# Moving softmax weights by small copies within SBUF, and splitting the keys' rotary product between GpSimd and an accumulating DMA

## The chip, the cores and the metric

The kernel runs on one core of a Trainium2 chip. The core has TensorE (PE, matrix products into PSUM), VectorE (DVE), ScalarE (ACT), GpSimd (POOL) and SyncE (SP), which here only issues DMAs. Each engine takes its instructions in the order in which they stand in its own queue; semaphores order the engines among each other. The metric is the time of one execution on the device in microseconds, and the median over the runs is what is compared. All arithmetic is float32, apart from the attention masks.

## What is computed

The input is x, 2 sequences of 2048 tokens of 128 features. Four residual layers follow each other, each on a layer norm of x:

```python
x = x + attention_a(layernorm(x))   # softmax over the queries' axis of x xT, 2048 x 2048 per sequence
x = x + ffn(layernorm(x))           # two transformer layers
x = x + attention_b(layernorm(x))   # one weight per token, from similarity of q and k
x = x + ffn(layernorm(x))           # the same two transformer layers again
```

The change lies in `ffn`. Each of its two layers has eight heads of 64 features with windows of 64 tokens, and then a gated feed-forward of width 341. Cut to what matters:

```python
q, k, v = split(shift_token(x) @ wqkv)
q, k = l2norm(q) * qs, l2norm(k) * ks
q = q * cos * scale + rotate_half(q) * sin * scale
k = k * cos / scale + rotate_half(k) * sin / scale
sim = (8 * q) @ kT over own and previous window, masked
x = x + (softmax(sim) @ v) @ wo
x = x + (a * gelu(g)) @ w2 + b2     # a, g = split(layernorm(shift_token(x)) @ w1 + b1)
```

`rotate_half` swaps the halves of a head's features (the sign is in the table). The l2 norm is a factor per token and head, so it may be applied after the rotation.

## The kernel before

A call `op(engine, cost, fn, r=..., w=..., late=...)` (class `Program`, line 102) records one operation with what it reads and writes; nothing is issued yet. At the end `Program.run` (line 127) lays all operations out: it keeps a clock per engine, advances it by the costs written in the calls and by `TAIL`, a delay until a result counts as there, and gives each engine the ready operation with the lowest number, shifted by `late`. Buffers are handed out in the same pass from pools of fixed size (`sizes`, line 322): an operation is only placed when its buffers are free. The outcome is one fixed order per engine; the chip follows it whatever the real durations are. A DMA on SyncE's queue that waits for data therefore holds back the DMAs behind it.

Attention a of both sequences comes first (`first_norm`, `first_attention`). Then four passes of the transformer run, two repetitions for each of the two sequences, as a chain of ticks (class `Block`): a pass has 16 blocks of 128 tokens per layer, and the second layer follows the first at a distance of 6 blocks. In all there are 4 x 2 x 16 = 128 calls of `Attention.block`, and 32 feed-forwards on 512 tokens.

One call of `block` does this, with the lines of the profile:

- Line 551: SyncE loads the block's table of cosines and sines (256 KB) from DRAM. There are three buffers for tables.
- Line 559: TensorE projects q and k for 128 tokens into two banks of PSUM, `pq[0]` and `pq[1]`; line 566 projects v, and line 567 (ScalarE) copies v to SBUF. Lines 569 and 573: SyncE moves v's halves so that each window and its predecessor lie in one buffer.
- Line 582: ScalarE squares each bank. Lines 583 and 584: VectorE multiplies each bank by the cosines (into `t1`) and by the sines (into `t2`), so four products of 128 x 512 per block.
- Lines 587 to 593: sums of squares, and the reciprocal norm; lines 394 to 397 are its Newton step on GpSimd.
- Line 591: GpSimd adds `t2`, halves swapped, to `t1` (128 x 1024). Line 597: GpSimd multiplies by the norm.
- Lines 606 and 607: VectorE transposes q into `qT` and k into `kring`, a ring of three blocks of keys. Line 628: TensorE multiplies queries with their 96 keys. Where the window begins before the ring's first column, the 96 keys lie in two pieces and each product is issued as two. Line 637 adds the masks.
- Lines 649 to 666: the softmax; line 666 (GpSimd) scales the weights. Line 677: VectorE transposes them in squares of 32 into `xp`.
- Line 686: four DMAs write `xp` into a DRAM buffer `far`, each 32 partitions to three row blocks. Line 691: one DMA reads `far` back into `pT` (512 KB). There the weights stand with the keys in the partitions; what the four DMAs never write in `far` was set to zero at the start (`clear`, line 517).
- Line 702: TensorE multiplies with v; line 709 (ScalarE) copies out; line 715 is the output projection of two blocks, and lines 721 and 722 (VectorE) add it.

Of the kernel before, what the change touches and what calls it, by code (L numbers as in the profile page):

```python
# [72 lines left out]
class Program:  # L73
# [6 lines left out]
    TAIL = {"PE": 0.28, "DVE": 0.2, "ACT": 0.25, "POOL": 0.19, "SP": 2.0}  # L80
# [195 lines left out]
def hybrid_kernel(ctx: ExitStack, tc: tile.TileContext, I, out):  # L276
# [37 lines left out]
    kring = [fixed([P, 4, R * P], f"kring{l}") for l in range(DEPTH)]  # L314

    def vec(i, rows=P):
# [7 lines left out]
        "w": (1024, 0), "c": (512, 12), "v": (VW, 6), "v0": (VW, 5), "tab": (TW, 3),  # L324
        "s0": (514, 2), "s1": (514, 3), "s2": (514, 2), "s3": (514, 2), 
        "n": (64, 7), "m": (16, 12), "row": (P, 4),
# [3 lines left out]
    scratch = ctx.enter_context(tc.tile_pool(name="scratch", bufs=1, space=bass.MemoryType.DRAM))  # L330
    slots["far"] = [scratch.tile([4 * P, 256], F32, name=f"far{i}") for i in range(8)]
# [4 lines left out]
    for b in range(B):  # L336
# [5 lines left out]
        "xn0": [("w", part[4]), ("w", part[5])],  # L342
        "xn1": [("w", part[6]), ("w", part[7])],
        "xnT0": [("w", part[8]), ("w", part[9])],
# [9 lines left out]
    def load(dst, key, src):  # L354
        op("SP", load_time(dst), lambda: sp.dma_start(out=dst, in_=src), w=[key], late=121)
# [5 lines left out]
    def load_x():  # L361
        c = len(x_tok)
        xt = buf("c")
        x_tok.append(xt)
        op(
            "SP", 2.0,
            lambda: sp.dma_start(out=xt().rearrange("p (n d) -> p n d", d=C), in_=x_rows[:, c * BPC : (c + 1) * BPC, :]),
            w=[xt],
        )
# [20 lines left out]
    def newton(v, r, rows, n, src):  # L390

        a = buf(src)
        A, V, Q = (lambda: a()[0:rows, 0:n]), (lambda: v()[0:rows, 0:n]), (lambda: r()[0:rows, 0:n])
        op("POOL", 0.22, lambda: po_.tensor_tensor(A(), Q(), Q(), ALU.mult), r=[r], w=[a], late=30)
        op("POOL", 0.22, lambda: po_.tensor_tensor(A(), A(), V(), ALU.mult), r=[v, a], w=[a], late=-30)
        op("POOL", 0.22, lambda: po_.tensor_scalar(A(), A(), -0.5, 1.5, ALU.mult, ALU.add), r=[a], w=[a], late=61)
        op("POOL", 0.22, lambda: po_.tensor_tensor(Q(), Q(), A(), ALU.mult), r=[r, a], w=[r])
# [13 lines left out]
    def first_norm(b, xn, xnT):  # L411
        for c in range(NCH):
# [9 lines left out]
            op("DVE", dve(512), lambda xg=xg, mean=mean: dv.tensor_reduce(row(mean), xg(), AX.X, ALU.add), r=[xt], w=[mean], late=56)  # L422
            op("DVE", 0.17, lambda mean=mean: dv.tensor_scalar(row(mean), row(mean), 1.0 / C, None, ALU.mult), w=[mean])
            op("DVE", dve(512), lambda xg=xg, ng=ng, mean=mean: dv.tensor_tensor(ng(), xg(), wide(mean), ALU.subtract), r=[xt, mean], w=[(xn, c)])
            op("ACT", act(512), lambda sq=sq, nf=nf: ac.activation(sq()[:, 0:CH], nf(), AF.Square), r=[(xn, c)], w=[sq])
            op("DVE", dve(512), lambda s3=s3, v=v: dv.tensor_reduce(row(v), s3(), AX.X, ALU.add), r=[sq], w=[v], late=84)
            op("DVE", 0.17, lambda v=v: dv.tensor_scalar(row(v), row(v), 1.0 / C, LN_EPS, ALU.mult, ALU.add), w=[v])
            op("ACT", 0.25, lambda v=v, r=r: ac.activation(row(r), row(v), AF.Ln), r=[v], w=[r], act="E", late=69)
            op("ACT", 0.25, lambda r=r: ac.activation(row(r), row(r), AF.Exp, scale=-0.5), w=[r], act="E", late=-36)
            newton(v, r, P, BPC, "m")  # L430
            op("DVE", dve(512), lambda ng=ng, r=r: dv.tensor_tensor(ng(), ng(), wide(r), ALU.mult), r=[r], w=[(xn, c)], late=-175)
            pt = transposes(BPC, (xn, c), lambda k, c=c: xn()[:, c * CH + k * P : c * CH + (k + 1) * P])
            op("ACT", act(512), lambda pt=pt, c=c: ac.copy(xnT()[:, c * CH : (c + 1) * CH], pt()), r=[pt], w=[(xnT, c)], late=-108)
            pt = transposes(BPC, xt, lambda k, xt=xt: xt()[:, k * P : (k + 1) * P])
            gc = b * NCH + c
            op("ACT", act(512), lambda pt=pt, gc=gc: ac.copy(xT[:, gc * CH : (gc + 1) * CH], pt()), r=[pt], w=[(xT_, gc)], late=-78)

    def first_attention(b, xn, xnT):
# [6 lines left out]
        for m in range(NBLK):  # L445
            group, z, xs = m // BPC, buf("m"), buf("row")
            e = [buf("e" if j <= group else "c" if j < NCH - 1 else "er") for j in range(NCH)]
            for j in range(group):
# [6 lines left out]
                op("PE", 0.115 * BPC, turned, r=[ident_] + [right[j * BPC + k, group] for k in range(BPC)], w=[pt], claim=[e[j]], late=-150)  # L455
                op("DVE", dve(512), lambda pt=pt, z=z, j=j: dv.tensor_reduce(z()[:, j : j + 1], pt(), AX.X, ALU.add), r=[pt], w=[(z, j)])
                op("ACT", act(512), lambda pt=pt, x=e[j]: ac.copy(x(), pt()), r=[pt], w=[e[j]])
            for j in range(group, NCH):
                sc = buf("p1")
                op("PE", pe(512), lambda sc=sc, m=m, j=j: pe_.matmul(out=sc(), lhsT=xnT()[:, m * P : (m + 1) * P], rhs=xnT()[:, j * CH : (j + 1) * CH], start=True, stop=True), r=[(xnT, group), (xnT, j)], w=[sc], claim=[e[j]], late=-79)  # L460
                op("ACT", act(512) + 0.25, lambda sc=sc, x=e[j], z=z, j=j: ac.activation(x(), sc(), AF.Exp, bias=shift, accum_out=z()[:, j : j + 1]), r=[sc], w=[e[j], (z, j)], act="E", late=-203)
                if j > group:
                    right[m, j] = e[j]
            op("DVE", 0.16, lambda z=z: dv.tensor_reduce(z()[:, 4:5], z()[:, 0:NCH], AX.X, ALU.add), w=[z])
            op("DVE", 0.17, lambda z=z: dv.reciprocal(z()[:, 4:5], z()[:, 4:5]), w=[z], late=-98)
            op("DVE", 0.3, lambda z=z, xs=xs, m=m: dv.tensor_scalar(xs(), xn()[:, m * P : (m + 1) * P], z()[:, 4:5], None, ALU.mult), r=[z, (xn, m // BPC)], w=[xs], late=-239)
            for j in range(NCH):
                op("PE", pe(512), lambda x=e[j], xs=xs, m=m, j=j: pe_.matmul(out=acc[j](), lhsT=xs(), rhs=x(), start=(m == 0), stop=(m == NBLK - 1)), r=[e[j], xs], w=[acc[j]], late=-32)  # L468
        for j in range(NCH):
            gc = b * NCH + j  # L470
            cols = xT[:, gc * CH : (gc + 1) * CH]
            op("DVE", dve(512), lambda cols=cols, j=j: dv.tensor_tensor(cols, acc[j](), cols, ALU.add), r=[acc[j]], w=[(xT_, gc)], late=-4)


    def center(src, keys):
# [3 lines left out]
        op("PE", pe(512), lambda: pe_.matmul(out=mp(), lhsT=meanw, rhs=src(), start=True, stop=True), r=keys, w=[mp], claim=[d, sq], late=-33)  # L479
        op("DVE", dve(512), lambda: dv.tensor_tensor(d(), src(), mp(), ALU.subtract), r=keys + [mp], w=[d], late=36)  # L480
        op("ACT", act(512), lambda: ac.activation(sq()[:, 0:CH], d(), AF.Square), r=[d], w=[sq], late=-31)
        op("PE", pe(512), lambda: pe_.matmul(out=vp(), lhsT=meanw, rhs=sq()[:, 0:CH], start=True, stop=True), r=[sq], w=[vp], claim=[r])  # L482
        op("ACT", act(512) + 0.1, lambda: ac.activation(r(), vp(), AF.Ln, bias=eps), r=[vp], w=[r], act="E", late=27)
        op("ACT", act(512), lambda: ac.activation(r(), r(), AF.Exp, scale=-0.5), w=[r], act="E", late=-27)
# [4 lines left out]
    def halo(s, before):  # L489
        if before is None:  # L490
            op("POOL", 0.15, lambda: po_.memset(s()[64:128, 0:1], 0.0), w=[(s, "h")], late=-49)
        else:
            op("POOL", 0.15, lambda: po_.tensor_copy(s()[64:128, 0:1], before()[64:128, CH : CH + 1]), r=[(before, BPC - 1)], w=[(s, "h")])
# [8 lines left out]
    def state_norm(gc, s, before):  # L502
        d, r = center(lambda: xT[:, gc * CH : (gc + 1) * CH], [(xT_, gc)])
        op("POOL", pool(512), lambda: po_.tensor_tensor(s()[0:64, 0:CH], d()[0:64, :], r()[0:64, :], ALU.mult), r=[d, r], w=[(s, k) for k in range(BPC)], late=-49)
        op("POOL", pool(512), lambda: po_.tensor_tensor(s()[64:128, 1 : CH + 1], d()[64:128, :], r()[64:128, :], ALU.mult), r=[d, r], w=[(s, k) for k in range(BPC)], late=-146)
# [7 lines left out]

    nought = Fixed()

    def clear():
        for far in slots["far"]:
            for a in range(4):
                z0 = a * P + (0 if a % 2 else 96)
                op("SP", 0.4, lambda far=far, z0=z0: sp.dma_start(out=far[z0 : z0 + 32, :], in_=I["zero"]), w=[(nought, z0)], late=7)  # L520

# [3 lines left out]
    def tables():  # L525
        for i in range(NBLK):
            raw = buf("tab")
            op("SP", 0.4, lambda i=i, raw=raw: sp.dma_start(out=raw(), in_=I["rot"][i]), w=[raw])
            for l in range(DEPTH):
# [6 lines left out]
                    r=[raw, qs_], w=[tab], late=35,  # L536
                )
                op("SP", 0.4, lambda l=l, i=i, tab=tab: sp.dma_start(out=turns[l][i], in_=tab()), r=[tab], w=[turns_[l][i]])

    class Attention:  # L540
# [4 lines left out]
        def block(self, i, s, s_out, before_out):  # L545
# [5 lines left out]
            op("SP", 0.4, lambda: sp.dma_start(out=tab(), in_=turns[l][i]), r=[turns_[l][i]], w=[tab], late=-48)  # L551
# [9 lines left out]
            for k in range(2):  # L561
                op("PE", 0.97, lambda k=k: project(k), r=keys_of(s, q) + [wqkv_], w=[pq[k]], claim=[sq, t1, t2], late=-24)
# [3 lines left out]
            op("PE", 0.885, lambda: pe_.matmul(out=pv(), lhsT=h(), rhs=wqkv[:, l, 2 * INNER : 3 * INNER], start=True, stop=True), r=keys_of(s, q) + [wqkv_], w=[pv], claim=[v])  # L566
            op("ACT", act(512), lambda: ac.copy(v(), pv()), r=[pv], w=[v], late=-123)  # L567
            old = self.v
            op("SP", 0.4, lambda: sp.dma_start(out=v0()[64:128, :], in_=v()[0:64, :]), r=[v], w=[(v0, 0)], late=71)
# [540 lines left out]
```

## Time and profile before

| | |
|---|---|
| median of 3 runs | 1640.41 us (1636.79 to 1644.73) |
| the profiled execution | 1623.37 us, of which the span is 1621.3 us |
| mean granted TensorE clock | 0.96 |
| busy: PE / DVE / ACT / POOL | 1482.7 / 1341.4 / 960.0 / 1072.2 us |
| share of the span | 91% / 83% / 59% / 66% |
| instructions: PE / DVE / ACT / POOL | 21659 / 2464 / 2426 / 1308 |
| DMA, all queues | 208.55 MB in 183542 packets, mean 129 GB/s |

The span runs from the first to the last instruction. Busy times are of one execution. The end of a matmul is modelled in the profile and consecutive matmuls overlap, so a busy TensorE is not one at its peak. A row of a group gives line, engine, operation, output and input, their shapes and the count, then the busy time and the mean duration of one, then the idle time before it with what ended it. "SPq" is SyncE's queue: its rows are the times in which DMAs are issued, not moved; the DMA list gives size and the median time from issue to landing. The first attention takes the first 200 us or so, the passes of the transformer nearly all the rest.

### The profile page before, as it was taken

Reading aid. Unit: us, or ns where it says so; the run is one execution under the profiler, and the core shown is the slowest. Engines: PE = TensorE matmul, PEld = TensorE weight load, DVE = VectorE, ACT = ScalarE, POOL = GpSimd, SP = SyncE. Lnnn points to the kernel's source line nnn. Section 1 sums busy time; section 2 is a strip of 40 time slices with the busy share of each in tenths; the row PEclk is TensorE's granted clock in tenths of the full one; section 3 lists DMA queues with packets and bytes.
Section 4 is the critical chain, followed back from the end, with each engine's and each line's share of the span. In section 5 each row is a group of like instructions: output and inputs, shape, how many; then the busy total and the mean of one; then the engine's idle time right before and its main releaser. Section 6 shows DMA issues by size and latency. Waiting matters only on the chain.

```text
span 1621.3 us, 53049 instructions
## 1 busy us (share of the span) xinstructions
PE 1482.7 (91%) x21659; PEld 844.0 (52%) x21659; DVE 1341.4 (83%) x2464; ACT 960.0 (59%) x2426; POOL 1072.2 (66%) x1308
## 2 busy tenths in 40 slices
PE   7999997989999999699999899799999999899875
PEld 4454554545555555355555464455555555555543
DVE  4533378799999899989998999989999989899772
ACT  6453455566666566465666666556666756566652
POOL 3440147578697767758687757758697877786561
PEclk9999998999999999799999999789999999999997
DMA  5540025455464543235555443255555555555432
GB/s 191 163 148 1 14 67 142 111 150 156 136 172 124 156 134 97 84 98 167 144 144 164 118 137 105 58 153 152 147 153 169 154 147 157 139 152 153 133 97 60
DMA packets 183542, 208.55 MB, mean 129 GB/s; under 512 B 18474, under 2 KB 143876, under 8 KB 183300
## 3 DMA queue, kind: packets, MB, share of 16 engines
q1 hardware_dynamic: 183300, 205.18, 44.4%
q8 instruction: 170, 2.79, 0.7%
q14 instruction: 72, 0.59, 0.1%
HBM read 111.78 MB, written 61.87 MB: 107 GB/s over the span
## 4 chain that ended last, share of the span: by engine, by line
PE 60%; DVE 17%; DMA 9%; POOL 5%; issue 4%; SPq 2%; ACT 2%; POOLq 0%; DVEq 0%; ACTq 0%
PE pp L751 9%; PE pp L559 9%; PE pp L702 6%; PE pp L628 6%; PE pp L715 5%; PE pp L468 5%; PE pp L566 5%; PE pp L776 4%; DMA arena<-far 3%; PE pp L482 2%; PE pp L479 2%; PE pp L460 2%; DMA right<-far 2%; DVE b_m L660 2%; DMA far<-arena 2%
## 5 line engine op out<-in xcount | busy, mean ns | idle before, releaser
L559 PE MATMUL pp<-wqkv,b_s 128*32 128x256 f32 x4096 | 263.4, 389 | 3.3 <-DVE arena L584 1.6
L654 ACT ACTIVATE arena<-pp,b_m 128x96 f32<-128x96 f32 x776 | 198.6, 363 | 92.2 <-DVE b_m L649 88.8
L666 POOL TENSOR_TENSOR arena<-arena,b_m 128x384 f32<-128x384 f32 x194 | 156.5, 827 | 91.1 <-DVE b_m L661 47.7
L751 PE MATMUL pp<-b_c,w 128*128 128x512 f32 (+1 forms) x384 | 176.8, 609 | 10.0 <-POOL b_c L747 7.8
L559 PEld LDWEIGHTS pp<-wqkv,b_s 128*32 128x32 f32 x4096 | 115.9, 110 | 129.8 <-issue 29.8
L628 PE MATMUL pp<-kring,b_c 64*32 64x96 f32 (+2 forms) x9728 | 150.2, 245 | 17.5 <-DVE kring L607 8.9
L628 PEld LDWEIGHTS pp<-kring,b_c 64*32 64x32 f32 x9728 | 121.5, 109 | 76.2 <-issue 33.6
L597 POOL TENSOR_TENSOR arena<-arena,b_n 128x1024 f32<-128x1024 f32 x80 | 152.9, 1913 | 3.5
L649 DVE TENSOR_REDUCE b_m<-pp 128x4 f32<-128x384 f32 x256 | 131.2, 540 | 18.8 <-PE pp L637 17.5
L566 PE MATMUL pp<-wqkv,b_s 128*128 128x512 f32 x256 | 143.8, 650 | 2.6 <-DVE b_n L589 2.6
L591 POOL TENSOR_TENSOR arena<-arena 128x1024 f32<-128x1024 f32 x51 | 120.9, 2370 | 36.4 <-DVE arena L584 28.5
L582 ACT ACTIVATE arena<-pp 128x512 f32<-128x512 f32 x170 | 100.9, 605 | 57.7 <-PE pp L559 49.9
L751 PEld LDWEIGHTS pp<-b_c,w 128*128 128x128 f32 (+1 forms) x384 | 67.3, 181 | 104.4 <-issue 72.4
L702 PE MATMUL pp<-arena,b_v 128*64 128x64 f32 x2560 | 96.1, 230 | 25.0 <-DMA arena<-far 14.1
L702 PEld LDWEIGHTS pp<-arena,b_v 128*64 128x64 f32 x2560 | 85.3, 143 | 61.0 <-issue 34.0
L584 DVE TENSOR_TENSOR arena<-pp,b_tab 128x512 f32<-128x512 f32 x172 | 114.0, 673 | 0.2
L583 DVE TENSOR_TENSOR arena<-pp,b_tab 128x512 f32<-128x512 f32 x160 | 105.7, 671 | 9.2 <-ACT arena L582 6.3
L567 ACT COPY b_v<-pp 128x512 f32<-128x512 f32 x128 | 75.7, 594 | 54.0 <-PE pp L566 53.8
L587 DVE TENSOR_REDUCE b_n<-arena 128x32 f32<-128x1024 f32 x85 | 101.8, 1198 | 1.7 <-ACT arena L582 1.7
L709 ACT COPY arena<-pp 128x512 f32<-128x512 f32 x80 | 47.6, 595 | 84.0 <-PE pp L702 82.0
L660 DVE TENSOR_REDUCE b_m<-arena 128x8 f32<-128x768 f32 x97 | 90.5, 933 | 7.3 <-ACT arena L654 6.9
L597 POOL TENSOR_TENSOR right<-right,b_n 128x1024 f32<-128x1024 f32 x48 | 92.3, 1923 | 2.3
(213 smaller groups left out, 3390.5 us busy)
## 6 DMA issues: line engine op xcount, KB each, us to landing
arena<-far SPq DMA_DIRECT2D x80, 512.0 KB, 4.2
far<-arena SPq DMA_DIRECT2D x344, 96.0 KB, 1.9
b_tab<-turn SPq DMA_DIRECT2D x128, 256.0 KB, 3.0
b_v<-b_v SPq DMA_DIRECT2D x248, 128.0 KB, 2.6
right<-far SPq DMA_DIRECT2D x48, 512.0 KB, 4.1
far<-right SPq DMA_DIRECT2D x168, 96.0 KB, 2.5
turn<-b_tab SPq DMA_DIRECT2D x32, 256.0 KB, 2.0
b_tab<-in_rot_dram SPq DMA_DIRECT2D x16, 256.0 KB, 2.8
```

The source lines that it names most:

```text
L559: pe_.matmul(out=pq[k]()[c * 32 : c * 32 + 32, a * 256 : (a + 1) * 256], lhsT=s()[:, at : at + 32], rhs=wqkv[:, l, c * 256 : (c + 1) * 256 ...
L566: op("PE", 0.885, lambda: pe_.matmul(out=pv(), lhsT=h(), rhs=wqkv[:, l, 2 * INNER : 3 * INNER], start=True, stop=True), r=keys_of(s, q) + ...
L584: op("DVE", dve(512), lambda part3=part3, src=src, trig=trig: dv.tensor_tensor(part3(t2), src(), trig(1), ALU.mult), r=[pq[k], tab], w=[(t ...
L591: op("POOL", pool(1024), lambda: po_.tensor_tensor(halves(t1), halves(t1), halves(t2)[:, :, ::-1, :], ALU.add), r=[t2], w=[t1], late=47)
L597: lambda: po_.tensor_tensor(t1().rearrange("p (h d) -> p h d", d=32), t1().rearrange("p (h d) -> p h d", d=32), nr()[:, 0:32].unsqueeze(2) ...
L628: pe_.matmul(out=sim[par]()[a * 32 : a * 32 + 32, pair * 96 + c0 : pair * 96 + c0 + n], lhsT=qT()[rows, pair * P + a * 32 : pair * P + a * ...
L649: op("DVE", dve(384), lambda sim3=sim3, mx=mx: dv.tensor_reduce(mx(), sim3(), AX.X, ALU.max, negate=True), r=[sim[par]], w=[(nm, par)])
L654: ac.activation(p()[:, hd * 96 : (hd + 1) * 96], sim[par]()[:, k * 96 : (k + 1) * 96], AF.Exp, bias=nm()[:, hd : hd + 1])
L660: op("DVE", dve(768), lambda: dv.tensor_reduce(rs()[:, 0:HEADS], p3(), AX.X, ALU.add), r=[p], w=[rs])
L666: lambda hs=hs: po_.tensor_tensor(p3()[:, hs, :], p3()[:, hs, :], rs()[:, hs].unsqueeze(2).to_broadcast([P, 4, 96]), ALU.mult),
L702: pe_.matmul(out=av()[par * 64 : par * 64 + 64, pair * P + w * WIN : pair * P + (w + 1) * WIN].rearrange("p (a c) -> p a c", a=2), lhsT=(v ...
L751: op("PE", pe(512), lambda: pe_.matmul(out=p_()[0:n, :], lhsT=w1[:, l, off + j * P : off + j * P + n], rhs=d(), start=True, stop=True), r= ...
```

## The change

Three things change in `block`, and with them the pools and the order.

1. *The sine product of the second bank.* ScalarE copies `pq[1]` to SBUF (`raw`), squares it from there, and GpSimd multiplies `raw` by the sines. VectorE keeps the sine product of the first bank and both cosine products. The product is written with its halves already swapped.
2. *The sum.* GpSimd's addition of 128 x 1024 is replaced by a DMA from GpSimd's queue that adds `t2` onto `t1` in SBUF.
3. *The softmax weights.* `far`, its four writes, the read and the zero filling are gone. Twelve DMAs on SyncE's queue copy squares of 32 partitions x 256 columns (32 KB) from `xp` to `pT`. `pT` now has a pool of its own of four buffers, out of the space of the first attention's tiles of the first sequence, filled with zeros where nothing is copied by four GpSimd instructions at the end of that attention.

Also, `kring` gets 64 columns in front of its three blocks. After each third block a DMA copies the ring's last 64 keys there, so that only a sequence's first block has its keys in two pieces.

The pools: `c` 12 to 10 buffers, `v` 6 to 7, `s1` 3 to 2, `n` 7 to 8, `m` 12 to 8, `row` 4 to 7, and 14 instead of 18 of kind `w` (1024 columns). `late` is another number in most calls, and `TAIL` of SP is 2.6 in place of 2.0, so the order of all queues differs.

```diff
-                op("ACT", act(512), lambda k=k, cols=cols: ac.activation(sq()[:, cols], pq[k](), AF.Square), r=[pq[k]], w=[(sq, k)], late=-5)
-                op("DVE", dve(512), lambda part3=part3, src=src, trig=trig: dv.tensor_tensor(part3(t1), src(), trig(0), ALU.mult), r=[pq[k], tab], w=[(t1, k)], late=-44)
-                op("DVE", dve(512), lambda part3=part3, src=src, trig=trig: dv.tensor_tensor(part3(t2), src(), trig(1), ALU.mult), r=[pq[k], tab], w=[(t2, k)])
+                if k:
+                    raw = buf("c")
+                    raw4 = lambda raw=raw: raw().rearrange("p (n a s d) -> p n a s d", n=4, a=4, s=2)
+                    op("ACT", act(512), lambda raw=raw: ac.copy(raw(), pq[1]()), r=[pq[1]], w=[raw], late=169)
+                    op("ACT", act(512), lambda raw=raw, cols=cols: ac.activation(sq()[:, cols], raw(), AF.Square), r=[raw], w=[(sq, k)], late=105)
+                    op("POOL", 1.25, lambda raw4=raw4, swap=swap, sin=sin: po_.tensor_tensor(swap(t2), raw4(), sin(), ALU.mult), r=[raw, tab], w=[(t2, k)], late=131)
+                else:
+                    op("ACT", act(512), lambda cols=cols: ac.activation(sq()[:, cols], pq[0](), AF.Square), r=[pq[0]], w=[(sq, k)])
+                    op("DVE", dve(512), lambda bank4=bank4, swap=swap, sin=sin: dv.tensor_tensor(swap(t2), bank4(), sin(), ALU.mult), r=[pq[0], tab], w=[(t2, k)])
+                op("DVE", dve(512), lambda k=k, part3=part3, bank=bank, cos=cos: dv.tensor_tensor(part3(t1), bank(), cos(), ALU.mult), r=[pq[k], tab], w=[(t1, k)], late=-47)
...
-            op("POOL", pool(1024), lambda: po_.tensor_tensor(halves(t1), halves(t1), halves(t2)[:, :, ::-1, :], ALU.add), r=[t2], w=[t1], late=47)
+            op("POOL", 0.9, lambda: po_.dma_start(out=t1(), in_=t2(), accum_op=ALU.add), r=[t2], w=[t1], tail=5.8, late=129)
...
+            if slot == R - 1:
+                op("SP", 0.4, lambda: sp.dma_start(out=ring[:, :, 0:WIN], in_=ring[:, :, R * P : WIN + R * P]), r=[(ring_, slot)], w=[(ring_, "before")], tail=3.0, late=-23)
...
             for a in range(4):
-                op(
-                    "SP", 0.4,
-                    lambda a=a, z0=a * P + 32 * (a % 2): sp.dma_start(
-                        out=far()[z0 : z0 + 96, :].rearrange("(n k) c -> k n c", k=32), in_=xp()[a * 32 : a * 32 + 32, 0:768].rearrange("k (n c) -> k n c", n=3)
-                    ),
-                    r=[xp, nought], w=[(far, a)], tail=3.2, late=85,
-                )
-            op("SP", 0.4, lambda: sp.dma_start(out=pT().rearrange("p (a c) -> p a c", a=4), in_=far().rearrange("(a p) c -> p a c", a=4)), r=[far], w=[pT], tail=3.6, late=40)
+                for n in range(3):
+                    z0 = 32 * (a % 2 + n)
+                    op(
+                        "SP", 0.37,
+                        lambda a=a, n=n, z0=z0: sp.dma_start(out=pT()[z0 : z0 + 32, a * 256 : (a + 1) * 256], in_=xp()[a * 32 : a * 32 + 32, n * 256 : (n + 1) * 256]),
+                        r=[xp], w=[(pT, 3 * a + n)], tail=2.2, late=44,
+                    )
```

## The prediction

> **What bounds the kernel now.** I read the busy time by stretches first, then the groups of that stretch, then the chain of waits, and last the timelines of TensorE and of SyncE's queue. The transformer layers fill the middle of the span; the stretch from 250 to 1550 us stands for them. Its columns are the length, then the busy us of PE, weight load, DVE, ACT and POOL, the granted clock, the DMA share and GB/s.
>
> ```profile
> core 0: us, PE busy (x) PEld busy (x) DVE busy (x) ACT busy (x) POOL busy (x), PEclk, DMA share, GB/s
> 250.00:1550.00 1300.00, 1197.60 (x19869) 693.69 (x19868) 1194.36 (x2137) 808.23 (x2060) 964.08 (x1168) 0.96 0.49 138
> ```
>
> VectorE works 1194.4 of 1300 us (91.9%), TensorE as much (92.1%), GpSimd 74%, ScalarE 62%. In this stretch GpSimd's line 591 ran 122 times, so I count 122 of the 128 blocks in it. TensorE's figure needs a correction, since matmuls overlap. Its timeline where it hardly stops gives start-to-start times:
>
> ```profile
> 1213.31 1.15 PE L702 MATMUL pp<-arena,b_v 128*64 128x64 f32 x32
> 1214.39 0.93 PE L628 MATMUL pp<-kring,b_c 64*32 64x96 f32 x60
> ...
> 1215.43 1.12 PE L479 MATMUL pp<-b_s,meanw 128*128 128x512 f32 x2
> 1216.48 1.24 PE L628 MATMUL pp<-kring,b_c 64*32 64x64 f32 x90
> ...
> 1217.85 1.12 PE L566 MATMUL pp<-wqkv,b_s 128*128 128x512 f32 x2
> ```
>
> Scores with their masks take 1.04 us (1214.39 to 1215.43), or 1.37 us where keys are cut in two (1216.48 to 1217.85); the values' product weighted by attention (line 702) takes 1.08. With 1.87 for the two projections of line 559, 0.96 for line 566, 0.3 for line 588 and 0.92 for line 715 from the same timeline, a block costs about 6.3 us: 122 of them 769 us, some 30 feed-forwards at 9.95 us (5.35 + 2.66 + two means of 0.97) 299 us, the rest about 80. So TensorE has some 1148 us of true work (88%) beside VectorE's 1194: VectorE leads by a little. The chain of waits says the opposite:
>
> ```profile
> PE 60%; DVE 17%; DMA 9%; POOL 5%; issue 4%; SPq 2%; ACT 2%; POOLq 0%; DVEq 0%; ACTq 0%
> ```
>
> Both are right: two engines near 90% with fixed orders wait for each other in turn. A gain on one is worth only part of its size.
>
> **The change, part by part.** These rows carry the prices (busy, mean ns, idle before):
>
> ```profile
> L597 POOL TENSOR_TENSOR arena<-arena,b_n 128x1024 f32<-128x1024 f32 x80 | 152.9, 1913 | 3.5
> L591 POOL TENSOR_TENSOR arena<-arena 128x1024 f32<-128x1024 f32 x51 | 120.9, 2370 | 36.4 <-DVE arena L584 28.5 <-DVE b_m L661 3.7 <-issue 3.2
> L584 DVE TENSOR_TENSOR arena<-pp,b_tab 128x512 f32<-128x512 f32 x172 | 114.0, 673 | 0.2
> L567 ACT COPY b_v<-pp 128x512 f32<-128x512 f32 x128 | 75.7, 594 | 54.0 <-PE pp L566 53.8
> L747 POOL TENSOR_TENSOR b_c<-b_c,b_c 128x512 f32<-128x512 f32 x32 | 40.8, 1276 | 23.8 <-ACT b_c L484 18.7 <-DVE b_m L660 4.2 <-POOL b_s L493 0.7
> ```
>
> *VectorE.* One of two sine products per block goes: 122 x 0.673 = 82 us, leaving 1112.
>
> *TensorE.* Keys no longer break at the ring's start, so 5 of 16 blocks lose 0.33 us: 40 x 0.33 = 13 us over the run, leaving about 1135. TensorE now leads.
>
> *ScalarE.* One copy out of PSUM per block, 122 x 0.594 = 72 us: 880 of 1300 (68%). The square of that half now waits for the copy, 0.6 us later; the sum of squares behind it is hidden while other blocks' work stands in VectorE's queue, and costs 0.6 us a block where it isn't.
>
> *GpSimd.* The 2.37 us addition goes; a 512-wide product (1.28, line 747's row) and the issue of a DMA come. No row shows GpSimd issuing one: from below SyncE's 0.3, from above 2.4, the addition it replaces. I take 1.0. The change is 122 x (1.28 + 1.0 - 2.37) = -11 us: 953 (73%).
>
> *The accumulating DMA.* It is waited for by the multiplication by the norm (line 597's work), in GpSimd's own queue, and by all behind it there: the softmax scaling, later Newton steps, and so VectorE's transposes. How long until it lands? Nearest row: a plain 512 KB transfer, 4.2 us. The Trainium skill, "DMA: Bandwidth & Descriptors", in "Anatomy of one DMA", fits a GpSimd-issued DMA at 2.0 us plus bytes/436 GB/s: 3.2 us here. Neither has the reading of the destination; twice the row, 8.4, is my upper end. I take 5.5. Against this stands the cover that the order gives: adding the durations above for all GpSimd instructions that the new program puts between each such DMA and its consumer gives 7.9 us in the median, under 5.2 us in 26 of 128. The shortfall, summed over the run, is 83 us for a landing of 6.5 and 33 for 5.2 if GpSimd never paused, 35 and 15 if it pauses as now (74% busy). So about 30 us at 5.5, in an engine with 350 us free; I let a third reach the others: +10 us. By the skill's 3.2 it would be nothing. I keep the row.
>
> *Softmax weights' move.* Now SyncE issues four writes to DRAM and one read back; the new program issues twelve copies within SBUF.
>
> ```profile
> 1195.29 1.77 SPq L686 DMA_DIRECT2D far<-arena  x4
> 1199.44 0.34 SPq L551 DMA_DIRECT2D b_tab<-turn  x1
> 1199.96 0.38 SPq L691 DMA_DIRECT2D arena<-far  x1
> ...
> 1232.49 0.47 SPq L569 DMA_DIRECT2D b_v<-b_v  x1
> 1233.01 0.59 SPq L573 DMA_DIRECT2D b_v<-b_v  x1
> ```
>
> ```profile
> arena<-far SPq DMA_DIRECT2D x80, 512.0 KB, 4.2
> far<-arena SPq DMA_DIRECT2D x344, 96.0 KB, 1.9
> b_v<-b_v SPq DMA_DIRECT2D x248, 128.0 KB, 2.6
> ```
>
> Before: 1.77 + 1.9 + 0.38 + 4.2 = 8.3 us from transpose to landed. After: twelve issues at 0.30 (the shortest write) to 0.59 (the second of two SBUF copies), then 2.2 to 2.6: 5.8 to 9.7. I take 0.45, between the writes' median 0.43 and the copies' 0.47: 5.4 + 2.4 = 7.8, about as now. The same page's rules for kernel authors say to join small transfers, since under 64 KB a DMA is mostly overhead. With its fit a 32 KB copy is 2.1 us, 25 us for twelve in a row; the timeline shows four issued within 1.77 us, each landing about 2 us later, so overhead overlaps and only the issues add. I follow the timeline.
>
> What the rule gets right is the queue. SyncE's DMAs in the layers go from 1016 to 1952 (1536 copies, 128 tables, 248 value halves, 40 copies of the ring's last 64 keys). At these issue times: 512 x 0.43 + 128 x 0.38 + 128 x 0.42 + 128 x 0.47 + 120 x 0.59 = 454 us before; after, 1536 x 0.45 + 54 + 60 + 71 + 40 x 0.45 = 894, of the 1395 us between the first projection (194) and the last block (1589): 33% becomes 64%. Behind each train of twelve (19 stand two or three in a row) wait tables, value halves and ring copies. Those have slack: in the page no DVE row waits for a table. I charge +3 us in all for trains beyond it, and nothing for the ring copies, needed a block later.
>
> *Without a price:* buffer counts and priorities move but add no work; 32 zero-filling DMAs give way to four GpSimd fills in the first 200 us, where GpSimd is idle two thirds of the time.
>
> **The sum.** Work of the leading engine goes from 1194 to 1135 us, with VectorE close behind at 1112. If it keeps 91.9%, the stretch is 1235 us (-65). If the new balance lets it reach no more than today's 87.3% (1135/1300), nothing is gained. The chain gives another figure: VectorE's 17% of 1621 is 276 us, of which 82/1194 are removed: 19 us. I take 90%: 1135/0.90 = 1261, -39. With +10 and +3: -26. The profiled execution took 1623.4 us (span 1621.3), so 1597; the median of the runs is 17 us higher than it, so **1614 us**.
>
> **The rivals.** 0.5% (8 us) is what a measurement can tell, so "no change" is 1632 to 1649.
>
> *Works as summed* (0.50): 1575 (no DMA charge, 91.9%) to 1632.
>
> *TensorE was the bound* (0.12): its near gapless timeline and the chain's 60% speak for it; VectorE's 96% in slices such as 400 to 480 us speaks against. The 26 us shrink to what the DMAs take back: about 1640.
>
> *SyncE's queue becomes the bound* (0.22), the case on the other side. In the new order each DMA waits for the one eight places earlier to land, so its pace is one eighth of a landing if that is longer than the issue. SyncE reaches VectorE's 92% when a DMA takes 0.92 x 1395/1952 = 0.66 us on average, a landing of 5.3 us; from there it decides. The rows show landings of 1.9 to 2.6, at most 6.5, against it; DMA share 0.49 and waits on data in its order speak for it. At 0.68: 1952 x 0.68/0.919 = 1444 us, +49: 1689.
>
> *The accumulation is slow* (0.16): landing in 10 us leaves 191 to 334 us uncovered, mean 262; GpSimd has 953 + 262 = 1215, at 91.9% 1322 us, +22, with SyncE's +3 in all +25: 1665. It decides from about 9.7 us, where GpSimd's sum passes today's 1194.
>
> **How the numbers follow.** Faster 0.50, same 0.12, slower 0.38. The range 1576 to 1695 reaches over both slow cases and leaves out about 2 in 10.
>
> **What would show it.** Right: sine products on VectorE halved to 128 at 0.67 us; VectorE near 88% and TensorE at or above 92% by the page's count between 250 and 1550; GpSimd's wait for the accumulating DMA under 40 us in all; small copies issued every 0.45 us. Wrong: copies at 0.65 us or more, TensorE's line 702 work waiting on them for over 60 us, or GpSimd's norm multiplication waiting over 200 us.

## The result and the profile after

The changed kernel takes 2004.78 us (median of 4 runs, 1998.73 to 2008.98) against 1639.43 (4 runs): a ratio of 1.222, with an interval of 1.217 to 1.227. The prediction was 1614, with a range from 1576 to 1695. The profiled execution took 1998.73 us, its span 1997.0. In the changed kernel line 698 holds the twelve small copies, 711 the product of weights and values (702 before), 600 the accumulating DMA, 606 the multiplication by the norm, 590 GpSimd's sine product, 593 and 594 VectorE's products.

The stretch from 250 to 1550 us, columns as before, and the shares of the chain of waits:

```profile
250.00:1550.00 1300.00, 1040.44 (x14676) 597.54 (x14668) 892.66 (x1605) 691.88 (x1718) 752.75 (x1029) 0.87 0.47 111
```

```profile
PE 37%; SPq 29%; DVE 12%; DMA 10%; issue 6%; POOL 3%; ACT 2%; POOLq 0%; DVEq 0%; ACTq 0%
```

No engine is near 90% any more: TensorE fell from 1197.6 to 1040.4 us, VectorE from 1194.4 to 892.7. SyncE's queue went from 2% of the chain to 29%, and its line 698 alone is 28% of it. The DMA engines are no busier than before (0.47, was 0.49). That points to the issuing of DMAs and not to the moving of data. The queue's timeline shows such issues (start, us, line, count):

```profile
1009.28 8.52 SPq L698 DMA_DIRECT2D arena<-arena  x12
...
1018.55 8.75 SPq L698 DMA_DIRECT2D arena<-right  x12
1027.41 9.16 SPq L698 DMA_DIRECT2D arena<-arena  x12
1036.67 0.68 SPq L619 DMA_DIRECT2D kring<-kring  x1
1037.46 0.57 SPq L567 DMA_DIRECT2D b_v<-b_v  x1
1038.08 0.59 SPq L571 DMA_DIRECT2D b_v<-b_v  x1
1038.77 0.53 SPq L549 DMA_DIRECT2D b_tab<-turn  x1
1039.40 7.53 SPq L698 DMA_DIRECT2D arena<-arena  x12
```

A train of twelve takes 7.5 to 9.2 us here, where four writes took 1.77. Three trains stand nearly back to back, and behind them the copies for the ring and for v, and a table. TensorE's timeline in the same microseconds, and then the waits of the whole run that name these copies (us in total, times, longest):

```profile
1035.10 0.34 PE L711 MATMUL pp<-arena,b_v 128*64 128x64 f32 x4 [2.23 <-DMA arena<-arena]
1037.95 1.76 PE L711 MATMUL pp<-arena,b_v 128*64 128x64 f32 x28 [2.52 <-DMA arena<-arena]
```

```profile
PE pp L711 <- DMA arena<-arena: 176.5, 75, 5.7
PE pp L711 <- DMA arena<-right: 125.1, 50, 6.7
...
POOL arena L590 <- DMA b_tab<-turn: 37.5, 6, 9.2
...
DVE arena L594 <- DMA b_tab<-turn: 23.6, 5, 8.7
```

The third train ends at 1036.57 and TensorE goes on at 1037.95, 1.4 us later, when the profile has its last copies landed. It waits 302 us in all for small copies, where the prediction called over 60 a sign of failure. (In the kernel before, it waited 25 us for the reads of `far`.) Tables come late too: GpSimd and VectorE wait 61 us for them in the two rows above, and the table at 1038.77 stands behind the three trains. The durations of one copy's issue (min/median/max in ns, first and last start):

```profile
L698 SPq DMA_DIRECT2D arena<-arena x972: 507/589/2642, 266.4 to 1955.5; - x195
```

The median is 0.589 us, not 0.45. From the start of one copy to the start of the next it is more: in the trace 1386 copies stand within 0.1 us behind another copy, and there the median step is 0.633 us and the mean 0.74, since some hold the queue for up to 2.6. In all, 245 of the 1536 hold it for over 0.65 us. They are frequent around the accumulating DMAs: 42% of the copies that start during the issue of one or within 3 us after it, and 8% of the others.

The parts of the change beside the copies cost, each by itself, about what was expected of them. The rows are GpSimd's sine product, its multiplication by the norm, and the accumulating DMA as issued (min/median/max) and landed (median us):

```profile
L590 POOL TENSOR_TENSOR arena<-b_c,b_tab 128x512 f32<-128x512 f32 x77 | 103.9, 1351 | 106.9 <-ACT b_c L588 42.0
...
L606 POOL TENSOR_TENSOR arena<-arena,b_n 128x1024 f32<-128x1024 f32 x69 | 135.6, 1975 | 4.4 <-DMA arena<-arena 1.9
...
arena<-arena POOLq DMA_DIRECT2D x40, 512.0 KB, 5.3
```

```profile
L600 POOL DMA_DIRECT2D arena<-arena x40: 627/877/1157, 233.8 to 1926.7; - x40
```

The multiplication waits 5.3 us in the whole run for the accumulation (1.9 here, 3.4 in its other row).

### The profile page after: what moved, and what is told of

It reads as the page before. It is cut to its first block, busy times and chain, and to the rows that moved or that the text cites. A ratio compares the mean times of both kernels' runs of the same rounds, so it can differ in the third digit from the quotient of the medians.

```text
span 1997.0 us, 52738 instructions
## 1 busy us (share of the span) xinstructions
PE 1605.8 (80%) x20379; PEld 908.9 (46%) x20379; DVE 1269.5 (64%) x2336; ACT 1033.7 (52%) x2554; POOL 1053.3 (53%) x1440
## 4 chain that ended last, share of the span: by engine, by line
PE 37%; SPq 29%; DVE 12%; DMA 10%; issue 6%; POOL 3%; ACT 2%; POOLq 0%; DVEq 0%; ACTq 0%
SPq L698 28%; PE pp L467 5%; PE pp L711 5%; DMA arena<-arena 5%; PE pp L557 4%; PE pp L459 3%; PE pp L724 3%; PE pp L760 3%; DMA arena<-right 3%; PE pp L785 3%; PE pp L564 2%; PE pp L638 2%; DVE b_m L659 1%; PE pp L488 1%; DVE arena L687 1%
## 5 line engine op out<-in xcount | busy, mean ns | idle before, releaser
L711 PE MATMUL pp<-arena,b_v 128*64 128x64 f32 x4096 | 212.8, 262 | 312.3 <-DMA arena<-arena 176.5
L711 PEld LDWEIGHTS pp<-arena,b_v 128*64 128x64 f32 x4096 | 180.7, 169 | 379.1 <-issue 247.7
L664 ACT ACTIVATE arena<-pp,b_m 128x96 f32<-128x96 f32 x576 | 144.9, 360 | 50.1 <-DVE b_m L659 46.3
L676 POOL TENSOR_TENSOR arena<-arena,b_m 128x384 f32<-128x384 f32 x144 | 117.4, 843 | 94.2 <-DVE b_m L671 60.2
L590 POOL TENSOR_TENSOR arena<-b_c,b_tab 128x512 f32<-128x512 f32 x77 | 103.9, 1351 | 106.9 <-ACT b_c L588 42.0
L676 POOL TENSOR_TENSOR right<-right,b_m 128x384 f32<-128x384 f32 x112 | 91.0, 833 | 85.5 <-DVE b_m L671 66.8
L664 ACT ACTIVATE right<-pp,b_m 128x96 f32<-128x96 f32 x448 | 112.7, 360 | 37.7 <-DVE b_m L659 34.3
L594 DVE TENSOR_TENSOR arena<-pp,b_tab 128x512 f32<-128x512 f32 x138 | 91.7, 677 | 60.3 <-DMA b_tab<-turn 23.6
L393 POOL TENSOR_TENSOR b_n<-b_n 128x32 f32<-128x32 f32 x128 | 36.8, 291 | 174.9 <-ACT b_n L602 167.6
L590 POOL TENSOR_TENSOR right<-b_c,b_tab 128x512 f32<-128x512 f32 x51 | 67.3, 1320 | 77.6 <-ACT b_c L588 60.1
```

The lines of the kernel that those rows point to most:

```text
L590: op("POOL", 1.25, lambda raw4=raw4, swap=swap, sin=sin: po_.tensor_tensor(swap(t2), raw4(), sin(), ALU.mult), r=[raw, tab], w=[(t2, k)], ...
L664: ac.activation(p()[:, hd * 96 : (hd + 1) * 96], sim[par]()[:, k * 96 : (k + 1) * 96], AF.Exp, bias=nm()[:, hd : hd + 1])
L676: lambda hs=hs: po_.tensor_tensor(p3()[:, hs, :], p3()[:, hs, :], rs()[:, hs].unsqueeze(2).to_broadcast([P, 4, 96]), ALU.mult),
L711: pe_.matmul(out=av()[par * 64 : par * 64 + 64, pair * P + w * WIN : pair * P + (w + 1) * WIN].rearrange("p (a c) -> p a c", a=2), lhsT=(v ...
```

## The experiments

The theory after the result (Q in the expectations): each small copy holds SyncE's queue for about 0.6 us, and 1536 of them make that queue the bound. The rivals: the rest of the change (rotary split, accumulation, pools, order) makes the loss; the copies' bytes do; or the planner was only told a wrong cost. The kernel before was timed beside each group of experiments; its medians lay from 1635.8 to 1641.3. The diffs are shortened: three dots, and words in brackets, stand for code left out.

**One part at a time.** The first kernel has the changed kernel's copies, pools and priorities, with the rotary part of the kernel before:

```diff
-  op("POOL", 0.9, lambda: po_.dma_start(out=t1(), in_=t2(), accum_op=ALU.add), r=[t2], w=[t1], tail=5.8, late=129)
+  op("POOL", pool(1024), lambda: po_.tensor_tensor(halves(t1), halves(t1), halves(t2)[:, :, ::-1, :], ALU.add), r=[t2], w=[t1], late=47)
   (and both squares from PSUM, both sine products on VectorE)
```

> The changed kernel with the rotary part of before: both sine products on VectorE and GpSimd's addition, no accumulating DMA. The twelve small copies, their pool and the ring's 64 columns stay. Theory Q (SyncE's queue is the bound, since each small copy occupies it 0.635 us from start to start, 975 us in all): as slow as the changed kernel, 1900 to 2050 us. Theory A (the accumulating DMA and the rotary split slow the rest, the copies included, by sharing the DMA engines): most of the loss is gone, 1640 to 1720 us.

Measured: 1994.44 us, ratio 1.220 (1.214 to 1.226). The copies, with the new pools and order, bring the whole loss without split and accumulation, at a DMA share of 0.27 in the stretch. Only 91 copies hold the queue for over 0.65 us here, where no DMA accumulates, and all issues of copies sum to 965 us instead of 1061. The time falls by 10 us alone: the queue's sum is not the only thing that sets it, and VectorE's part of the chain is larger here. The chain:

```profile
PE 37%; SPq 26%; DVE 17%; DMA 8%; issue 6%; ACT 3%; POOL 3%; DVEq 0%; POOLq 0%; ACTq 0%
```

The second kernel, called the rotary kernel below, is the complement: `far`, its four writes, its read and 18 buffers of kind `w` come back, the rest of the change stays.

```diff
-  for n in range(3): op("SP", 0.37, lambda ...: sp.dma_start(out=pT()[z0 : z0 + 32, ...], in_=xp()[...]), ...)
+  op("SP", 0.4, lambda ...: sp.dma_start(out=far()[z0 : z0 + 96, :]..., in_=xp()[...]), ...)
+  op("SP", 0.4, lambda: sp.dma_start(out=pT()..., in_=far()...), r=[far], w=[pT], ...)
```

> The changed kernel with the softmax weights moved as before (four writes to DRAM, one read back, 18 buffers of 1024 columns); the rotary split, the accumulating DMA and the ring's 64 columns stay. Theory Q: the loss is gone, and what the prediction summed without the copies holds, 1590 to 1635 us. Theory A: 1850 us or more.

Measured: 1755.16 us, 1.072 (1.067 to 1.077). The loss of the copies is gone, but neither theory had 1755. There must be a second cause, which the changed kernel does not show; its experiments follow those on the copies.

**The number of copies.** Six of twelve are left out (so half of the weights are missing), everything else in the changed kernel's own order:

```diff
-  lambda ...: sp.dma_start(out=pT()[...], in_=xp()[...])
+  lambda ...: (a + n) % 2 or sp.dma_start(out=pT()[...], in_=xp()[...])
```

> The changed kernel in its own order, but six of the twelve copies of each block are left out, so that part of the weights' tile holds old numbers. Theory Q: 768 x 0.635 = 488 us less in SyncE's queue, which is then no longer the bound: 1600 to 1720 us. Theory O (the order itself, planned with 0.37 us a copy and with new priorities, is bad, whatever the queue does): above 1850 us.

Measured: 1626.93 us (one run), with 1635.84 before beside it. Stretch and chain:

```profile
250.00:1550.00 1300.00, 1189.51 (x18714) 685.80 (x18718) 1115.11 (x2016) 869.83 (x2176) 939.85 (x1288) 0.96 0.54 123
```

```profile
PE 51%; DVE 18%; DMA 9%; SPq 7%; POOL 6%; issue 5%; ACT 3%; POOLq 0%; DVEq 0%; ACTq 0%
```

TensorE is back at 91.5%, the clock at 0.96, and VectorE at 1115 us: the prediction said 1112. Pools, order, split and the whole accumulation are those of the changed kernel, so none of them makes the loss by itself. Next, twenty-four copies of half the size:

```diff
-  sp.dma_start(out=pT()[z0 : z0 + 32, a * 256 : (a + 1) * 256], ...)
+  [sp.dma_start(out=pT()[z0 : z0 + 32, a * 256 + c : a * 256 + c + 128], ...) for c in (0, 128)]
```

> The changed kernel in its own order, each copy split into two of 128 columns: the same bytes in 24 copies per block. Theory Q: 1536 x 0.635 = 975 us more in a queue that is already the bound, 2900 to 3100 us. Theory B: near 2005 us.

Measured: 2934.39 us (one run), within Q's band.

```profile
SPq 60%; PE 19%; issue 10%; DVE 4%; DMA 4%; POOL 2%; ACT 1%; POOLq 0%; DVEq 0%; ACTq 0%
```

The bytes are the same and the copies 1536 more: (2934.4 - 2004.8)/1536 = 0.605 us for each. From six to twelve it is (2004.8 - 1626.9)/768 = 0.49; a smaller step is to be expected if the queue binds only above six. The opposite test halves each copy's bytes at the old number, so half of the weights are missing again:

```diff
-  out=pT()[z0 : z0 + 32, a * 256 : (a + 1) * 256]
+  out=pT()[z0 : z0 + 32, a * 256 : a * 256 + 128]     (in_ likewise)
```

> The changed kernel in its own order, each of the twelve copies moves 128 of its 256 columns (16 KB), so that half of the weights' tile holds old numbers. Theory Q (issue time per copy, whatever its size): 1960 to 2020 us. Theory B (bytes or the DMA engines' load): halfway to before, about 1820 us.

Measured: 1954.32 us (one run), 50 less and a little under Q's band; the issue's median stays 589 ns. Half the bytes give 50 us back; half the number, and half the bytes with it, gave 378.

**The cost of an issue by itself.** Behind the last work of the kernel before, trains of DMAs are issued on an otherwise idle chip, with one kind per train (one run; the kernel's total of 1728 us says nothing).

```diff
...
+  for k in range(16): sp.dma_start(out=arena[32:64, 2048 + k*256 : 2304 + k*256], in_=arena[32:64, 0:256])   # L1004; L1002: other partitions
+  for k in range(16): sp.dma_start(out=arena[32:64, 6144 + k*256 : 6160 + k*256], in_=arena[0:32, 256:272])  # L1006: 2 KB
+  for k in range(16): sp.dma_start(out=arena[:, 2048 + k*256 : 2304 + k*256], in_=arena[:, 512:768])         # L1008: 128 KB
+  for k in range(16): sp.dma_start(out=far[...], in_=arena[0:32, 0:256])                                     # L1010: to DRAM
...
+  for k in range(16): sp.dma_start(out=arena[32:64, ...], in_=far[1][0:32, :])                               # L1014: from DRAM
+  for k in range(16): ac.dma_start(...)                                                                      # L1017: ScalarE's queue
...
```

> The kernel before, with trains of DMAs behind its end while nothing else runs: 16 copies of 32 x 256 from partitions 0-31 to 32-63, 16 within the same partitions, 16 of 32 x 16, 16 of 128 x 256, 16 writes of 32 x 256 to DRAM, 6 of the old form (32 x 3 x 256), 16 reads of 32 x 256 from DRAM, 16 copies from ScalarE's queue, 8 accumulations of 128 x 1024. Theory Q (issuing a copy within SBUF costs the queue about 0.6 us, whatever its size): 0.57 to 0.61 us each for all four copy forms on the idle chip too. Theory B (the 0.59 is back pressure of busy DMA engines or of eight copies in flight): 0.47 or less on the idle chip, and less for 32 x 16 than for 128 x 256. Writes to DRAM: 0.30 to 0.45 by both.

SyncE's timeline, and the durations of one issue in two of the trains (min/median/max in ns):

```profile
1639.33 10.12 SPq L1004 DMA_DIRECT2D arena<-arena  x16
1649.55 10.04 SPq L1006 DMA_DIRECT2D arena<-arena  x16
1659.63 10.25 SPq L1008 DMA_DIRECT2D arena<-arena  x16
1669.92 7.55 SPq L1010 DMA_DIRECT2D far<-arena  x16
...
1680.38 7.40 SPq L1014 DMA_DIRECT2D arena<-far  x16
```

```profile
L1004 SPq DMA_DIRECT2D arena<-arena x16: 588/589/598, 1639.3 to 1648.9; - x16
L1010 SPq DMA_DIRECT2D far<-arena x16: 419/419/586, 1669.9 to 1677.0; - x16
```

Sixteen copies within SBUF take 10.0 to 10.25 us, 0.63 to 0.64 each, with 2 KB, 32 KB or 128 KB; with DRAM on one side 7.4 to 7.55, 0.46 to 0.47 each. The medians of the issues themselves are 584 to 599 ns and 419 ns, at landings of 1.6 to 2.1 us. So the usual pace of a train goes with the form of the DMA (within SBUF, or with DRAM on one side), not with its size, and it needs no traffic beside it. The long issues of the running kernel don't occur here: the longest of SyncE's copies within SBUF takes 601 ns.

**Order or number.** The planner is told 0.66 us per copy:

```diff
-  "SP", 0.37,
+  "SP", 0.66,
```

> The changed kernel, planned with 0.66 us for a small copy in place of 0.37; the same work in another order. Theory Q: the queue's work stays at 975 us for the copies and some 230 us for the rest in about 1400 us, so only part comes back: 1780 to 1950 us. Theory O (the loss is the plan's wrong cost): 1640 to 1700 us.

Measured: 1928.34 us, ratio 1.176 (1.169 to 1.184). An order planned with the measured cost gives 76 of 365 us back: the wrong cost in the plan is about a fifth. In the next kernel the copies with n = 1, four of twelve, go through ScalarE's queue (cost written 0.65 for all):

```diff
+  who, q_ = ("ACT", ac) if n == 1 else ("SP", sp)
-  "SP", 0.37, lambda ...: sp.dma_start(...)
+  who, 0.65, lambda ...: q_.dma_start(...)
```

> The changed kernel with four of the twelve copies issued from ScalarE's queue, all planned at 0.65 us. Theory Q: 325 us leave SyncE's queue for a ScalarE that is idle for more than that: 1650 to 1760 us. Theory B (the DMA engines' load): the transfers are the same, 1900 us or more.

Measured: 1820.14 us, 1.110 (1.103 to 1.118), 108 less than the 1928 with nearly the same planned cost and the same transfers: the direction is Q's, and the size was missed, as it lies over the 1650 to 1760 of Q.

```profile
PE 31%; DVE 19%; DMA 18%; SPq 9%; ACT 7%; issue 7%; POOL 6%; ACTq 2%; DVEq 0%; POOLq 0%
```

SyncE's part of the chain fell to 9% while DMAs' landings rose to 18%, so the next wait is for landings; which of them binds was not tested.

**The second cause.** What made the rotary kernel 1755? First its frame: its ring, pools and priorities, with the rotary part of the kernel before.

```diff
-  (raw copy, GpSimd's sine product, accumulating DMA)
+  (four products on VectorE, GpSimd's addition of the swapped halves)
```

> The second run's kernel with the rotary part of before as well: what is left of the change is the ring's 64 columns, the pools and the new priorities. Theory D (in the second run the accumulating DMA's traffic delays the round trip by DRAM): 1620 to 1660 us. Theory P (the new priorities and pools fit only the new form of the kernel): 1700 us or more.

Measured: 1659.87 us, 1.011 (1.002 to 1.020), so the frame costs some 20 of the 119 us (3 to 33 by the interval). Beside the 1994 us of the first kernel of this section, it leaves 335 us to the copies. Then the reverse: split and accumulation in the kernel before, with its own pools and priorities (A), and the split alone there, the sum left to GpSimd (B):

```diff
   (squares, raw copy and products as in the change; then)
+  op("POOL", 0.9, lambda: po_.dma_start(out=t1(), in_=t2(), accum_op=ALU.add), ...)               # A
+  op("POOL", pool(1024), lambda: po_.tensor_tensor(t1(), t1(), t2(), ALU.add), ..., late=47)       # B
```

> The kernel before, its own pools and priorities, with the rotary split and the accumulating DMA alone. Theory D: the loss of the second run remains, 1700 to 1790 us. Theory P: 1600 to 1650 us.

> As the run before it, but GpSimd adds the two products (128 x 1024, 2.4 us) and no DMA accumulates. VectorE loses its 82 us in the middle stretch; GpSimd gains 122 x 1.28 = 156 us and stands at 1120 of 1300. Theory D: the DMA traffic is as before, so 1610 to 1650 us, the split's gain against a fuller GpSimd. If GpSimd's load is what costs: 1660 us or more.

Measured: 1858.00 us (1.132) for A and 1747.61 us (1.065) for B, A slower than either theory had it, and B where GpSimd's load was to put it. B has no accumulation at all, so in the old frame the split by itself costs 108 us; the difference of the two, 110 us, goes with the accumulation in place of GpSimd's addition. The same two parts in the new frame, one at a time:

```diff
-  (k = 1: raw copy on ScalarE, sine product on GpSimd)
+  op("DVE", dve(512), lambda ...: dv.tensor_tensor(swap(t2), bank4(), sin(), ALU.mult), ...)      # accumulation only
```

```diff
-  op("POOL", 0.9, lambda: po_.dma_start(out=t1(), in_=t2(), accum_op=ALU.add), ..., tail=5.8, late=129)
+  op("POOL", pool(1024), lambda: po_.tensor_tensor(t1(), t1(), t2(), ALU.add), ..., late=129)     # split only
```

> The second run's kernel with both sine products on VectorE: the accumulating DMA without the split. Theory D: the traffic is all there, 1720 to 1770 us. Theory P: nearer to the ninth run, 1640 to 1690 us.

> The second run's kernel with GpSimd's addition in place of the accumulating DMA: the split alone, with the new priorities. Theory D: no extra traffic, 1610 to 1670 us. If the split itself costs (GpSimd fuller, one copy more in the chain): 1700 to 1760 us.

Measured: 1785.43 us (1.088) with the accumulation only, 1673.39 (1.020) with the split only, each a little above D's band. With weights through `far` and the new frame that makes a square: neither 1660, split 1673, accumulation 1785, both 1755. The accumulation costs 82 to 126 us. The split costs 13 without it, which the intervals (1.002 to 1.020, and 1.014 to 1.025) don't separate from nothing, and gives 30 back with it. In B the same split with the same work on GpSimd cost 108 us, so most of that goes with the old frame and not with GpSimd's load; which part of it (the order, the pools or the missing ring copy) stays open.

What does the accumulation cost time by: its own landing, or what its data does to others? The last kernel is the rotary kernel, same order, with only 64 of 1024 columns accumulated, so most of the rotary sum is missing:

```diff
-  po_.dma_start(out=t1(), in_=t2(), accum_op=ALU.add)
+  po_.dma_start(out=t1()[:, 0:64], in_=t2()[:, 0:64], accum_op=ALU.add)
```

> The second run's kernel (rotary split and accumulating DMA, weights by DRAM) in its own order, but the accumulating DMA adds only 64 of the 1024 columns (32 KB in place of 512), so that most of the rotary sum is missing. Theory D (the accumulation's traffic delays the other transfers): the 95 us between the second and the ninth run come back, 1650 to 1690 us. Theory P (order and longer chains, not bytes): 1720 to 1760 us.

Measured: 1604.18 us, 0.977 (0.971 to 0.984), 151 us less than with all columns, and more than D expected to come back. The rotary kernel with all columns: its stretch, its queue of accumulations (packets, MB, share of the 16 engines), landings (median us) and waits.

```profile
250.00:1550.00 1300.00, 1126.33 (x17148) 652.02 (x17152) 1030.39 (x1857) 799.76 (x2006) 869.83 (x1198) 0.92 0.70 175
```

```profile
q0 software_dynamic: 18432, 67.12, 20.9%
```

```profile
far<-arena SPq DMA_DIRECT2D x372, 96.0 KB, 3.1
b_tab<-turn SPq DMA_DIRECT2D x128, 256.0 KB, 4.2
b_v<-b_v SPq DMA_DIRECT2D x248, 128.0 KB, 4.0
arena<-arena POOLq DMA_DIRECT2D x56, 512.0 KB, 6.3
```

```profile
PE pp L713 <- DMA arena<-far: 74.0, 26, 9.9
...
PE pp L713 <- DMA right<-far: 49.6, 17, 8.0
...
POOL arena L607 <- DMA arena<-right: 11.2, 5, 6.1
```

The same with 64 columns:

```profile
250.00:1550.00 1300.00, 1204.77 (x18888) 692.22 (x18888) 1131.09 (x2041) 882.84 (x2211) 954.36 (x1317) 0.97 0.55 147
```

```profile
q0 software_dynamic: 18432, 4.20, 3.0%
```

```profile
far<-arena SPq DMA_DIRECT2D x372, 96.0 KB, 2.2
b_tab<-turn SPq DMA_DIRECT2D x128, 256.0 KB, 3.3
b_v<-b_v SPq DMA_DIRECT2D x248, 128.0 KB, 2.8
```

```profile
PE pp L713 <- DMA arena<-far: 19.2, 15, 2.9
...
PE pp L713 <- DMA right<-far: 16.2, 8, 7.4
```

The multiplication that needs the accumulation (line 607) waits 15.5 us for it in all, 11.2 of that in the row shown, and 3.9 with 64 columns; nothing else waits for it. So its own landing is not the loss. The landings of others are late: with all columns a write to `far` lands in 3.1 us instead of 2.2, v's halves in 4.0 instead of 2.8, a table in 4.2 instead of 3.3 (the read of `far` hardly changes, 4.7 and 4.6). TensorE waits 124 us for the reads of weights instead of 35, as a read stands behind its writes. The packets are as many in both kernels; their bytes and the time that they take differ, and the DMA engines' share is 0.70 against 0.55. It is what the accumulation moves, beside `far`, that costs the time.

## Why the prediction was wrong

*The step that failed first* is "I take 0.45" for the issue of a small copy, and with it "I charge +3 us in all" for the trains. In a train a copy takes 0.589 us to issue, and 0.74 goes by per copy in the running kernel; where +3 us was charged, TensorE alone waits 302. The 0.45 lay between 0.43, the median of the writes, which go to DRAM, and 0.47, the median of v's first half, which stays within SBUF as the new copies do. The second half took 0.59. The kernel before has both:

```profile
L569 SPq DMA_DIRECT2D b_v<-b_v x128: 461/467/1635, 197.5 to 1550.3; - x128
L573 SPq DMA_DIRECT2D b_v<-b_v x120: 461/590/1724, 198.0 to 1547.4; - x120
```

The two have the same size and form. In the trace they differ by what stands before them: 75 of the second halves are issued within 0.1 us behind the first half, and their median is 0.597; after a pause of over 0.3 us in the queue a half of either kind takes 0.467 in the median. A copy in a train stands behind another copy, so the second half was its likeness, and the prediction used it as the upper end only. The train with its landing was to last 7.8 us; in the rows shown it takes 7.5 to 9.2 before the last landing, and 27 where three follow each other.

*The rival that came true*, SyncE's queue as the bound, was named with 1689 us. Its point of decision, 0.66 us on average, was passed by the copies' 0.74; its reason, one eighth of a landing, was not what happened: the idle chip has the same 0.59 at landings near 2 us. Its size was wrong in two ways. With 0.74 for all 1952 DMAs its formula gives 1952 x 0.74/0.919 = 1572 us for the layers. They took some 1740, from the first DMA of the layers (226) to the last copies (1963): by this estimate the queue is filled to about 83% and not to VectorE's 92%, as it also waits in order for data. And the same matmuls took longer, 416 ns (line 557) instead of 389 (559), at a granted clock of 0.88 over the run instead of 0.96.

*The slack* that I gave tables and v's halves ("no DVE row waits for a table") held for a queue with trains of 1.8 us. Behind trains of 8 to 27 us tables are waited for over 60 us.

*The cost of twelve landings* was rightly set aside. The fit of the Trainium skill ("DMA: Bandwidth & Descriptors", "Anatomy of one DMA") is stated for DMAs that GpSimd issues, and the prediction put it to SyncE's copies as well. Its 2.1 us is near the 1.8 to 2.0 of a 32 KB copy on the idle chip; but landings overlap and issues add, so 25 us for twelve was no figure for a train.

*What was right.* VectorE's work: 1112 said, 1115 with six copies; TensorE in the lead by the page's count, 91.5 to 92.7% where 92 was said, once the queue or the traffic no longer bound. ScalarE's copy: 0.594 said, 0.588. The accumulation in the changed kernel: landing 5.5 said, 5.3 measured, where the skill's fit gave 3.2; its issue 1.0 said, 0.88; GpSimd's wait for it 5.3 us in all. The sum of the parts without any charge for DMAs was 1584 + 17 = 1601 us, and the kernel with 64 accumulated columns, where neither copies nor traffic bind, takes 1604. So near a match is partly luck, as that kernel moves its weights through `far` and has the 20 us of the frame in it. "Today's 87.3%" in the sum is a slip, since TensorE's share was 1148/1300, 88.3%; it had no part in the 1614.

*What was missing.* Two terms stood at nothing. "Buffer counts and priorities move but add no work": they cost some 20 us in the kernel that has only them, and in the old frame the split cost 108 that it doesn't cost in the new one. And I had priced the accumulation by its latency and not by what it moves, 67 MB (128 x 512 KB) for engines that were half busy. Beside `far`, at DMA shares of 0.63 to 0.70, this costs 82 to 151 us. In the changed kernel it hardly shows, 2005 us with split and accumulation against 1994 without; nor with six copies, where the whole accumulation stays at a share of 0.54 and the time is 1627. No kernel here has all the copies, their issue solved, and the accumulation.

No kernel that does the whole computation beat the one before.

## What to carry to other kernels

Count the DMAs that one queue issues and price each by a row of the same form (SBUF to SBUF is not SBUF to DRAM) and in the same place (directly behind another DMA, not after a pause), before looking at bytes: twelve small copies in place of five DMAs made this kernel 22% slower while the DMA engines were half idle. When an engine's sum is replaced by an accumulating DMA, its data can be a cost to other transfers even where hardly anything waits for it, so compare the landings of the other queues. A fixed order hides neither: what stands behind a long train in a queue comes late, as tables did here.

## What the runs showed of the hardware

- In a train, a plain DMA within SBUF holds the queue that issues it for 0.59 us, at 2, 32 and 128 KB alike and in the same partitions or others, and for 0.60 from ScalarE's queue; with DRAM on one side it is 0.42. After a pause in the queue it is less: 0.47 for v's halves in the kernel before. The Trainium skill, "DMA: Bandwidth & Descriptors", in "Issuing engines are not separate DMA queues", calls the sequencer's time for initiating a DMA usually small relative to the DMA itself. Here it is 0.59 beside a landing of about 2 us, and the landings overlap while the issues of one queue don't.
- Accumulating 512 KB in SBUF lands in about 5 to 7 us here (medians; 9.9 with eight issued one behind the other on the idle chip), and where the engines' share is 0.70 it lengthens those of other queues by a quarter to two fifths (2.2 to 3.1, 2.8 to 4.0, 3.3 to 4.2). In the changed kernel, of SyncE's copies that start during the issue of one or within 3 us after it, 42% hold their queue for over 0.65 us, of the others 8%.
- TensorE's granted clock was lower where it was idle more. In the stretch from 250 to 1550 us it was 0.96 at 92% busy before, 0.87 at 80% with the change, and 0.74 at 59% with twenty-four copies. That waits lower the clock agrees with "TensorE: Matmul & The Clock Gate" in the skill (in "Part 1: The HAM clock gate"), where activity releases the throttle; no run here changed one without the other.
